# Causal masks written into the score banks first, and AV moved ahead of other work, in a two-layer transformer block

## The chip, the cores and the metric

One core of a Trainium2 chip runs the whole program in one launch. The metric is device time in microseconds, the median of several executions. TensorE multiplies matrices into PSUM banks (eight of them, 128 partitions by 512 fp32 columns), VectorE and ScalarE read those banks, GpSimd and the DMA queues move and prepare data. Each engine works through its own list of instructions in the order in which the program was recorded, and waits for other engines by semaphores.

## What is computed

The input is 8 sequences of 512 tokens with 256 features. Layer 0 is a layer norm, unmasked attention and a routed expert network beside it. Layer 1, which the change is about, is a layer norm, a causal attention that runs twice, and a low-rank network beside it:

```python
q, k, v = (qkv[:, :, 0], qkv[:, :, 1], qkv[:, :, 2])   # 16 heads of 16 features
ctx = _causal_attn(q, k, v)                            # softmax(mask(q k^T / 4)) v
ctx_c = ctx.reshape(b, s, d).transpose(0, 2, 1)
conv_out = conv(ctx_c, conv_w, width 3) + conv_b
q2 = conv_out.transpose(0, 2, 1).reshape(b, s, NUM_HEADS, HEAD_DIM)
ctx2 = _causal_attn(q2, k, v)
out = ctx2.reshape(b, s, d) @ out_w.T + out_b
```

The convolution is written in short here. In the causal attention, key positions later than the query get minus infinity before the softmax.

## The kernel before

**Jobs.** The attention is cut into jobs of one sequence and four heads. Layer 1 has 64 jobs: 32 for the first attention (`firsts`) and 32 for the second (`seconds`), which come in turn, the second behind the first by LAG = 7. A head has 16 features in a row group of 32 partitions, so four heads fill the 128 rows of TensorE, and matmuls of different heads use different 32-row tiles of it.

**Steps.** A job takes six steps in layer 1 (STEPS), and `run` (L442) goes through all steps of all jobs in one line. In every step two things are under way. The newer job gets the row maxima of its scores (`scores`, L332): queries on the partitions, two heads per step, all in fp32, and VectorE takes the maxima out of the banks (L365). Twelve steps later (LEAD) the same job gets its scores again (`exps`, L384), this time with keys on the partitions and the maxima already subtracted (a spare row of q holds them, written by `shift`, L372, by a transpose L375 and four small DMAs on SP's queue). ScalarE takes the exponentials out (L421). The query blocks of the maxima (MX_SEQ) and the key blocks of the scores (SC_SEQ) are paired so that they have equal widths: 512, then 384 and 128 in one bank, then 256, and the same again for the other two heads. `zip` (L482) puts the maxima matmuls of two heads (L345) and the score matmuls of the other two (L394) side by side, so that all four row tiles have work.

**Masks.** Keys of block kc are only scored for queries from block kc on (L389), so only the first 128 columns of each piece need a mask. `after` (L407) adds it: one bf16 matmul per head (L412) of an identity with `mask_t`, which holds -1e30 above the diagonal, onto the first `len(blocks)*128` columns. The pieces lie in the bank such that the masked columns come first: the piece with offset 0 is 128 wide where there are two. In this matmul TensorE works as one array of 128 rows.

**AV.** `attend` (L427) multiplies exponentials by values (L434), with the four heads on four 32-column tiles of TensorE. By AV_AT a job attends its key block 0 in the sixth step of its scores, blocks 1 and 3 in the next (the first step of the following job), block 2 in the one after it. After the last, `l1_done` (L1101) has ScalarE copy the result (L1106), and books its transposes into token order (`to_tokens`, L1090), which VectorE divides (L1093, L1094).

**Other work.** Projections of q and k (L293, emptied by VectorE at L283 and by ScalarE at L285), values (L303, L311), transposes into features (L266; emptied at L268 by VectorE and L270 by ScalarE), the convolution (L1072, in two halves, emptied by VectorE at L283), the output projection (L1124, added by VectorE at L1131) and `to_tokens` are booked in a list (`Work`) with an earliest and a latest step. In layer 1 `fill` (L118) takes at most one of them per step, more only if they are due.

**Order in a step.** Maxima and scores, masks, exponentials (issued to ScalarE), `fill`, then `attend`.

**Banks.** In layer 1 the rings are: three banks for maxima ("mx"), three for scores ("sc"), one for AV, one for all other work ("mm"). A step takes two of the three "mx" and two of the three "sc" banks. For the last LEAD steps `banks_last` hands the banks of the maxima to the scores.

Of the kernel before, what the change touches and what calls it, by code (L numbers as in the profile page):

```python
# [1 line left out]

# [17 lines left out]
P = 128  # L20
NB = 8
S = 512
# [5 lines left out]
PH = 32  # L28
# [46 lines left out]
SC_SEQ = (  # L75
    [((i // 2,), 1 - i % 2) for i in range(8)],
    [((0,), 0), ((3, 1), 0), ((2,), 0), ((0,), 1), ((3, 1), 1), ((2,), 1)],
    [((0,), 0), ((0,), 1), ((3, 1), 0), ((3, 1), 1), ((2,), 0), ((2,), 1)],
)
# [73 lines left out]
def block_kernel(ctx: ExitStack, tc: tile.TileContext, x, a0_wqk, a0_bqk, a0_wv, a0_bv, cent, experts,  # L153
                 a1_wqk, a1_bqk, a1_wv, a1_bv, conv_w, conv_b, out_w, out_b, u1, v1, f_b1, u2, v2, f_b2, out):
    nc = tc.nc
# [20 lines left out]
    ident_bf = const.tile([P, P], BF16, name="ident_bf")  # L176
    nc.vector.tensor_copy(ident_bf, ident)

    mask_t = const.tile([P, 2 * P], BF16, name="mask_t")
# [19 lines left out]
    def share_banks(**kinds):  # L199

        rings.update({k: list(v) for k, v in kinds.items()})

    def bank(kind="mm"):
        rings[kind].append(rings[kind].pop(0))
        return rings[kind][-1]
# [5 lines left out]
    def banks_alone():  # L211
        share_banks(mx=banks[:3], sc=banks[3:6], av=banks[6:7], mm=banks[7:])


    def banks_last():
        share_banks(sc=banks[:5], av=banks[6:7], mm=banks[5:6] + banks[7:])
# [4 lines left out]
    class Norms:  # L221
# [4 lines left out]
        def __init__(self, pool, bs, nm, twice):  # L226
            self.bs, self.nm, self.twice = bs, nm, twice
            n = len(bs) * NC
            self.mv = pool.tile([P, n, 2], F32, name=f"mv{nm}", bufs=1)
            self.rs = pool.tile([P, 2 if twice else 1, n], F32, name=f"rs{nm}", bufs=1)  # L230
            self.rs1 = pool.tile([P, n], F32, name=f"rs1{nm}", bufs=1) if twice else None
            self.nm2 = pool.tile([P, n], F32, name=f"nn{nm}", bufs=1) if twice else None
            self.nm_t = pool.tile([P, n], F32, name=f"nm{nm}", bufs=1)
# [85 lines left out]
    class Job:  # L319


        def __init__(self, nm, causal, scale, v, g, done, pool):
            self.nm, self.causal, self.scale, self.v, self.g, self.done = nm, causal, scale, v, g, done
            self.pool = pool
            self.q = self.k = None
            self.m = None
            self.seq = int(causal)
            self.shift_row = (HD, 0)[g % 2]
            self.e = {}
            self.av = None  # L330

        def scores(self, i):  # L332
# [39 lines left out]
        def shift(self):  # L372
# [8 lines left out]
            for c in range(NC):  # L381
                nc.sync.dma_start(out=self.q[self.shift_row : P : PH, c * P : (c + 1) * P], in_=mT[4 * c : 4 * c + 4, :])

        def exps(self, i):  # L384
            blocks, pr = SC_SEQ[self.seq][i]
            heads = [bank("sc") for _ in range(2)]
            parts, at = [], 0
            for kc in blocks:
                lo = kc * P if self.causal else 0  # L389
                parts.append((kc, at, lo))  # L390
                at += S - lo
            mm = [
                [
                    lambda h=h, kc=kc, at=at, lo=lo: nc.tensor.matmul(  # L394
                        heads[h % 2][:, at : at + S - lo],
                        lhsT=self.k[h * PH : (h + 1) * PH, kc * P : (kc + 1) * P],
                        rhs=self.q[h * PH : (h + 1) * PH, lo:],
                        start=kc == blocks[-1],
                        stop=not self.causal,
                    )  # L400
                    for h in (2 * pr, 2 * pr + 1)
                ]
                for kc, at, lo in reversed(parts)
            ]
            n = at

            def after():  # L407
                if self.causal:


                    for h in range(2):
                        nc.tensor.matmul(  # L412
                            heads[h][:, : len(blocks) * P], lhsT=ident_bf, rhs=mask_t[:, : len(blocks) * P],
                            start=False, stop=True,
                        )
                e = self.pool.tile(
                    [P, 2, n], F32, tag=f"e{blocks[0]}" if self.causal else "e", name=f"e{self.nm}_{i}",
                    bufs=3 if self.causal else 4,
                )
                for h in range(2):  # L420
                    nc.scalar.activation(e[:, h, :], heads[h][:, :n], AF.Exp, scale=self.scale)  # L421
                for kc, at, lo in parts:
                    self.e[kc, pr] = e[:, :, at : at + S - lo]

            return mm, after
# [16 lines left out]
    def run(jobs, work_of, layer, per_step, most):  # L442
        steps, lead = STEPS[layer], LEAD[layer]
        end = steps * len(jobs)
        if layer == 1:
            for job in jobs[-(lead // steps) :]:
                job.seq = 2
        attends = {}
        for j, job in enumerate(jobs):
            av_at = AV_AT[job.seq]  # L450
            for i, blocks in av_at.items():
                attends.setdefault(lead + steps * j + i, []).append((job, blocks, i == max(av_at)))

        def attend(t):
            for job, blocks, last in attends.pop(t, ()):
                for kc in blocks:
                    job.attend(kc, kc == 0, last and kc == blocks[-1])
                if last:
                    job.done(job, t)

        work_of.first()
        for t in range(max(attends) + 1):
            work_of.t = t
            if layer == 0 and t == lead:
                banks_alone()
            mm, after = [], []
            if t >= lead or layer == 1:
                maxima = (t,)
            else:

                maxima = (t, t + 1) if t % 2 == 0 else ()

            scores = (t - lead,) if t < end else (t - lead, t - lead + 1) if (t - end) % 2 == 0 else ()
            if t == end:
                banks_last()
            for at, call in [(i, Job.scores) for i in maxima] + [(i, Job.exps) for i in scores]:
                j, i = divmod(at, steps)
                if 0 <= j < len(jobs):
                    m, a = call(jobs[j], i)
                    mm.append(m)  # L480
                    after.append(a)
            for together in zip(*mm):  # L482
                for m in together:
                    for f in m:
                        f()
            for f in after:
                f()
            work_of.fill(t, per_step, most)
            attend(t)
        work_of.drain()  # L490

    fgs, yns, norms_of = {}, {}, {}
# [72 lines left out]
    with ExitStack() as l0:  # L565
# [335 lines left out]
        jobs = []  # L901
# [37 lines left out]
        for i in range(2):  # L939
            norms[1].stats(i)  # L940
        todo.stream = stream()
        run(jobs, todo, 0, MOE_PER_STEP, 99)
        later.close()

# [16 lines left out]
    with tc.tile_pool(name="ffn", bufs=1, side="right", reuse_waits="tile") as ffn:  # L961
# [53 lines left out]
        for n, (b, c2) in enumerate(pairs):  # L1015
# [6 lines left out]
            _, _, hT = ahead.pop(0)  # L1022
# [11 lines left out]
    for i in range(2):  # L1034
        t = l1.tile([P, 2, S + 2], F32, tag=f"ctxT{i}", name=f"ctxT{i}", bufs=1)
# [107 lines left out]
    firsts, seconds, jobs = [], [], []  # L1143
# [30 lines left out]
    for n in range(NB * HG + LAG):  # L1174
        if n < NB * HG:
            l1_job(1, n)
        if n >= LAG:
            l1_job(2, n - LAG)
    run(jobs, todo1, 1, 99.0, 1)


# [86 lines left out]
```

## Time and profile before

| | |
|---|---|
| median of 3 runs | 2121.69 us (2117.05 to 2124.36) |
| the profiled execution | 2120.86 us |
| its span in the trace | 2118.7 us |
| TensorE busy (PE) | 2010.6 us, 95% of the span |
| VectorE (DVE), ScalarE (ACT) | 1228.6 us, 867.8 us |
| layer 1's attention | from about 1140 us to the end |
| maxima matmuls L345 | 3072 passes, 765.1 us busy (both layers) |
| score matmuls L394 | 3072 passes, 682.6 us busy (both layers) |
| mask matmuls L412 | 768, 123.4 us busy |
| AV matmuls L434 | 3072 passes, 317.8 us busy (both layers) |

An fp32 matmul of the program is two instructions of the profile (two passes), each with a weight load (PEld) ahead of it; a bf16 one is one. Busy times of matmuls that run side by side overlap, and a matmul's recorded end lies behind the time at which the next one may start, so a stretch that shows TensorE at 99% can still hold waits: they are found in the timeline and in the list of waits. "issue" as a releaser means that nothing shown by the profile was waited for.

### The profile page before, as it was taken

To read this page: it belongs to the slowest core of one execution; us is meant where nothing else is said; L and a number is where in the kernel's file an instruction comes from. 1 tells how busy PE (TensorE), PEld (TensorE's weight loads), DVE (VectorE), ACT (ScalarE), POOL (GpSimd) and SP (SyncE) were. 2 spreads that over 40 slices of the span, in tenths; PEclk is the share of its full clock that TensorE was granted. 3 is DMA by queue.
4 is the path that set the end of the run, shared out by engine and by line. 5 is a ranking of instruction groups with operands and counts; after the bars stand their busy time and mean duration, and the time that the engine had idled before them with its cause. 6 is when DMAs were issued, how large, how long until landed. Compare 5 with 4: busy or idle time off the path is not lost.

```text
span 2118.7 us, 35530 instructions
## 1 busy us (share of the span) xinstructions
PE 2010.6 (95%) x13672; PEld 1016.4 (48%) x13672; DVE 1228.6 (58%) x3565; ACT 867.8 (41%) x1690; POOL 175.6 (8%) x222
## 2 busy tenths in 40 slices
PE   5797999999999999998898999999999999999998
PEld 3333555555555555552233445455555545554554
DVE  5564455555555555557424676666766666666763
ACT  4342333333333333335551444444444444444434
POOL 4153000000000000004211000000000000000000
PEclk8698999999999999999999899999999999999999
DMA  6014212212121221202100000000000000000000
GB/s 211 13 45 143 104 54 105 101 58 105 53 105 53 105 105 53 105 11 78 40 1 1 2 2 2 2 2 12 2 12 2 12 2 12 2 11 2 2 12 21
DMA packets 37192, 93.53 MB, mean 44 GB/s; under 512 B 5920, under 2 KB 28064, under 8 KB 34080
## 3 DMA queue, kind: packets, MB, share of 16 engines
q0 software_dynamic: 6384, 59.78, 7.7%
q1 hardware_dynamic: 29792, 30.56, 4.5%
q8 instruction: 107, 1.75, 0.3%
q10 hardware_dynamic: 848, 0.93, 0.1%
q14 instruction: 61, 0.50, 0.1%
HBM read 70.03 MB, written 20.45 MB: 43 GB/s over the span
## 4 chain that ended last, share of the span: by engine, by line
PE 83%; DVE 6%; issue 5%; DMA 4%; ACT 2%; POOL 1%; ACTq 0%; POOLq 0%; DVEq 0%; SPq 0%
PE bank L345 27%; PE bank L434 12%; PE bank L794 8%; PE bank L815 8%; PE bank L293 5%; PE bank L1072 4%; PE bank L412 4%; DMA hs_d<-h,pos_i 4%; PE bank L394 3%; PE bank L303 2%; PE bank L1090 2%; PE bank L1124 1%; DVE m L362 1%; PE bank L977 1%; PE bank L990 1%
## 5 line engine op out<-in xcount | busy, mean ns | idle before, releaser
L421 ACT ACTIVATE e<-bank 128x512 f32<-128x512 f32 (+1 forms) x1280 | 638.9, 552 | 921.4 <-PE bank L394 462.8
L345 PE MATMUL bank<-k,q 32*128 32x512 f32 (+3 forms) x3072 | 765.1, 538 | 24.6 <-DVE m L362 20.3
L394 PE MATMUL bank<-q,k 32*128 32x512 f32 (+3 forms) x3072 | 682.6, 535 | 2.4 <-DVE m L362 1.6
L365 DVE CUSTOM_DVE_ANT_0 jk<-bank,cmask 128x512 bf16<-128x512 f32 (+3 forms) x1024 | 502.8, 491 | 241.7 <-PE bank L345 162.4
L345 PEld LDWEIGHTS bank<-k,q 32*128 32x128 f32 x3072 | 301.4, 187 | 388.4 <-issue 165.2
L362 DVE TENSOR_REDUCE m<-bank 128x1 f32<-128x512 f32 x512 | 328.8, 685 | 152.5 <-PE bank L394 122.7
L434 PE MATMUL bank<-e,v 128*32 128x512 f32 (+3 forms) x3072 | 317.8, 501 | 0.7 <-ACT e L421 0.7
L394 PEld LDWEIGHTS bank<-q,k 32*128 32x128 f32 x3072 | 266.0, 186 | 12.2 <-issue 6.1
L794 PE MATMUL bank<-hsT,w 128*128 128x256 f32 x736 | 181.2, 392 | 6.4 <-DVE hsT L777 6.4
L794 PEld LDWEIGHTS bank<-hsT,w 128*128 128x128 f32 x736 | 135.1, 192 | 74.5 <-issue 58.9
L815 PE MATMUL bank<-w,hT 128*128 128x256 f32 x736 | 170.7, 385 | 0.0
L815 PEld LDWEIGHTS bank<-w,hT 128*128 128x128 f32 x736 | 137.5, 192 | 36.6 <-issue 18.7
L434 PEld LDWEIGHTS bank<-e,v 128*32 128x32 f32 x3072 | 67.7, 108 | 139.7 <-issue 133.0
L412 PE MATMUL bank<-mask_t,ident_bf 128*128 128x128 bf16 (+1 forms) x768 | 123.4, 244 | 0.0
L412 PEld LDWEIGHTS <-ident_bf 128*128 128x128 bf16 x768 | 43.9, 97 | 155.7 <-issue 140.6
L807 DVE TENSOR_SCALAR hT<-bank,w 128x256 f32<-128x256 f32 x92 | 44.5, 484 | 113.7 <-ACT hT L805 113.7
L1072 PE MATMUL bank<-ctxT,cw_sb 128*128 128x256 f32 x384 | 90.0, 383 | 2.1 <-DVE q L283 1.8
L365 DVE DVE_READ_ACCUMULATOR2_ANT m<- 128x1 f32 x1024 | 85.0, 83 | 0.0
L805 ACT ACTIVATE hT<-bank,w 128x256 f32<-128x256 f32 x92 | 43.7, 475 | 92.9 <-PE bank L794 92.9
L824 DVE TENSOR_TENSOR f<-bank,w 128x256 f32<-128x256 f32 x46 | 19.5, 425 | 105.4 <-PE bank L815 105.4
L285 ACT ACTIVATE k<-bank,bqk,rows 128x512 f32<-128x512 f32 x64 | 46.3, 774 | 81.7 <-PE bank L293 72.4
L1072 PEld LDWEIGHTS bank<-ctxT,cw_sb 128*128 128x128 f32 x384 | 70.1, 189 | 13.2 <-DVE q L283 3.2
(186 smaller groups left out, 1383.5 us busy)
## 6 DMA issues: line engine op xcount, KB each, us to landing
q<-mT SPq DMA_DIRECT2D x384, 2.0 KB
hs_d<-zeros SPq DMA_DIRECT2D x23, 256.0 KB
hs<-hs_d SPq DMA_DIRECT2D x23, 256.0 KB
fs_d<-f SPq DMA_DIRECT2D x23, 256.0 KB
acc<-in_x SPq DMA_DIRECT2D x8, 512.0 KB
out<-acc SPq DMA_DIRECT2D x8, 512.0 KB
cw_sb<-in_conv_w SPq DMA_DIRECT2D x1, 768.0 KB
wqk<-in_a_wqk ACTq DMA_DIRECT2D x1, 512.0 KB
```

What stands on the lines that cost most here:

```text
L285: nc.scalar.activation(dst, ps, AF.Identity, bias=bias[:, half : half + 1], scale=rows[:, half : half + 1])
L293: nc.tensor.matmul(ps, lhsT=w[:, k, col : col + P], rhs=src[:, k, :], start=(k == 0), stop=(k == 1))
L345: lambda h=h, qc=qc, at=at, nk=nk: nc.tensor.matmul(heads[h % 2][:, at : at + nk], lhsT=self.q[h * PH : (h + 1) * PH, qc * P : (qc + 1) * ...
L362: nc.vector.tensor_reduce(self.m[:, qc, h, :], src, AX.X, ALU.max, negate=True)
L365: nc.vector.tensor_tensor_reduce(out=junk[:, :nk], in0=src, in1=cmask[:, S - nk :], scale=1.0, scalar=-3e38, op0=ALU.add, op1=ALU.max, acc ...
L394: lambda h=h, kc=kc, at=at, lo=lo: nc.tensor.matmul(heads[h % 2][:, at : at + S - lo], lhsT=self.k[h * PH : (h + 1) * PH, kc * P : (kc + 1 ...
L412: nc.tensor.matmul(heads[h][:, : len(blocks) * P], lhsT=ident_bf, rhs=mask_t[:, : len(blocks) * P], start=False, stop=True,)
L421: nc.scalar.activation(e[:, h, :], heads[h][:, :n], AF.Exp, scale=self.scale)
L434: nc.tensor.matmul(self.av[h * PH : (h + 1) * PH, lo:], lhsT=self.v[:, kc, 4 * self.g + h, :], rhs=es[h // 2][:, h % 2, :], start=first, s ...
L794: nc.tensor.matmul(ps[:, i * TB : (i + 1) * TB], lhsT=w[:, O_W1 + k * FF + fc * P : O_W1 + k * FF + (fc + 1) * P], rhs=self.hsT[:, k, :], ...
L815: nc.tensor.matmul(ps[:, 0:D], lhsT=self.hT[:, fc, j * P : (j + 1) * P], rhs=w[:, O_W2 + fc * D : O_W2 + (fc + 1) * D], start=(fc == 0), s ...
L1072: nc.tensor.matmul(ps[:, :w], lhsT=cw_sb[:, k, tap, c * P : (c + 1) * P], rhs=ctxT[b % 2][:, k, tap + lo : tap + lo + w], start=(k == 0 an ...
```

## The change

Three things change in layer 1.

First, `masks` (new) runs at the end of each step and takes the two score banks of the next step. It writes the mask into them with `start=True`, ahead of the scores; `exps` finds these banks by `self.banks`. The scores then add to them (`start=False`).

Second, since the mask covers only some columns of the bank, each score matmul is cut at the end of its masked columns: one 128-wide piece on masked columns, one for the rest. A 512-wide matmul becomes 384 and 128, a 256-wide one 128 and 128; 384 and 128 become 256, 128 and 128. The lists of maxima and scores now differ in length, so `zip` becomes `zip_longest`, and the last score pieces stand alone at the end. Per job that is 28 score matmuls in place of 16. The mask matmuls stay 12 per job.

Third, up to the last LEAD steps, `attend` comes ahead of `fill`. The order in a step is then: maxima and scores, exponentials, AV, other work, the masks of the next step. `banks_last` moves from the start of step `end` to the end of the step before it.

In layer 0 the instructions and their order stay what they were, and on every engine but TensorE layer 1's order stays too, except that ScalarE's copy of a finished AV is now issued ahead of the same step's other work.

```diff
+        def masks(self, i):
+            n = len(SC_SEQ[self.seq][i][0]) * P
+            self.banks[i] = heads = [bank("sc") for _ in range(2)]
+            for h in heads:
+                nc.tensor.matmul(h[:, :n], lhsT=ident_bf, rhs=mask_t[:, :n], start=True, stop=False)
+
         def exps(self, i):
             blocks, pr = SC_SEQ[self.seq][i]
-            heads = [bank("sc") for _ in range(2)]
+            heads = self.banks.pop(i) if self.causal else [bank("sc") for _ in range(2)]
...
+            pieces = [(kc, at, lo, S) for kc, at, lo in parts]
+            if self.causal:
+                pieces = [(kc, at, lo, lo + P) for kc, at, lo in parts]
+                pieces += [(kc, at + P, lo + P, S) for kc, at, lo in parts if lo + P < S]
             mm = [
                 [
-                    lambda h=h, kc=kc, at=at, lo=lo: nc.tensor.matmul(
-                        heads[h % 2][:, at : at + S - lo],
+                    lambda h=h, kc=kc, at=at, lo=lo, hi=hi: nc.tensor.matmul(
+                        heads[h % 2][:, at : at + hi - lo],
                         lhsT=self.k[h * PH : (h + 1) * PH, kc * P : (kc + 1) * P],
-                        rhs=self.q[h * PH : (h + 1) * PH, lo:],
-                        start=kc == blocks[-1],
-                        stop=not self.causal,
+                        rhs=self.q[h * PH : (h + 1) * PH, lo:hi],
+                        start=not self.causal,
+                        stop=at == 0,
                     )
                     for h in (2 * pr, 2 * pr + 1)
                 ]
-                for kc, at, lo in reversed(parts)
+                for kc, at, lo, hi in reversed(pieces)
             ]
...
             def after():
-                if self.causal:
-                    for h in range(2):
-                        nc.tensor.matmul(
-                            heads[h][:, : len(blocks) * P], lhsT=ident_bf, rhs=mask_t[:, : len(blocks) * P],
-                            start=False, stop=True,
-                        )
...
-            for together in zip(*mm):
+            for together in zip_longest(*mm, fillvalue=()):
                 for m in together:
                     for f in m:
                         f()
             for f in after:
                 f()
+            early = layer == 1 and t < end
+            if early:
+                attend(t)
             work_of.fill(t, per_step, most)
-            attend(t)
+            if not early:
+                attend(t)
+            if t + 1 == end:
+                banks_last()
+            for at in scores_at(t + 1) if layer == 1 else ():
+                j, i = divmod(at, steps)
+                if 0 <= j < len(jobs):
+                    jobs[j].masks(i)
```

`scores_at(t)` is the old expression for the steps whose scores belong to t, made a function.

More of the change, by code (lines that the diff above doesn't have):

```diff
@@ L1 @@
 from contextlib import ExitStack
+from itertools import zip_longest
 import concourse.bass as bass
@@ L329, in __init__ @@
             self.e = {}
+            self.banks = {}
             self.av = None
@@ L391, in exps @@
                 at += S - lo
+            n = at
+            pieces = [(kc, at, lo, S) for kc, at, lo in parts]
+            if self.causal:
+                pieces = [(kc, at, lo, lo + P) for kc, at, lo in parts]
+                pieces += [(kc, at + P, lo + P, S) for kc, at, lo in parts if lo + P < S]
             mm = [
                 [
-                    lambda h=h, kc=kc, at=at, lo=lo: nc.tensor.matmul(
-                        heads[h % 2][:, at : at + S - lo],
+                    lambda h=h, kc=kc, at=at, lo=lo, hi=hi: nc.tensor.matmul(
+                        heads[h % 2][:, at : at + hi - lo],
                         lhsT=self.k[h * PH : (h + 1) * PH, kc * P : (kc + 1) * P],
-                        rhs=self.q[h * PH : (h + 1) * PH, lo:],
-                        start=kc == blocks[-1],
-                        stop=not self.causal,
+                        rhs=self.q[h * PH : (h + 1) * PH, lo:hi],
+                        start=not self.causal,
+                        stop=at == 0,
                     )
@@ L402, in exps @@
                 ]
-                for kc, at, lo in reversed(parts)
+                for kc, at, lo, hi in reversed(pieces)
             ]
-            n = at
             def after():
-                if self.causal:
-                    for h in range(2):
-                        nc.tensor.matmul(
-                            heads[h][:, : len(blocks) * P], lhsT=ident_bf, rhs=mask_t[:, : len(blocks) * P],
-                            start=False, stop=True,
-                        )
                 e = self.pool.tile(
@@ L459, in attend, with scores_at @@
                     job.done(job, t)
+        def scores_at(t):
+            return (t - lead,) if t < end else (t - lead, t - lead + 1) if (t - end) % 2 == 0 else ()
         work_of.first()
@@ L471, in run @@
                 maxima = (t, t + 1) if t % 2 == 0 else ()
[L473 to L476, printed above, removed]
+            for at, call in [(i, Job.scores) for i in maxima] + [(i, Job.exps) for i in scores_at(t)]:
                 j, i = divmod(at, steps)
```

## The prediction

> **What bounds the kernel now.** I first read the busy time by stretches (engine columns are busy us and instruction counts), then the waits of the layer-1 stretch, then the timeline step by step.
>
> ```profile
> 1190.00:2085.00 895.00, 887.08 (x7706) 466.45 (x7698) 609.61 (x2275) 402.64 (x833) 0.00 (x0) 1.00 0.02 6
> ...
> PEld bank L345 <- DVE m L365: 55.8, 113, 0.8
> ...
> PEld bank L1090 <- ACT avs L1106: 11.1, 39, 0.4
> ```
>
> In steady layer 1 (1190 to 2085 us) TensorE is busy for 887 of 895 us, VectorE 610, ScalarE 403. ScalarE waits 431 us for the masks (L412), but that is slack: exponentials are read two or more steps later. What TensorE waits for is the maxima on VectorE (55.8 us), then the copied AV or a freed work bank. The prize is small: everything TensorE waits for in layer 1 is some 80 to 90 us, and masks and scores keep their columns.
>
> The timeline repeats every six steps with only a few kinds of each, so I measured each kind's length from the slot of one mask pair to the next (the slot follows the last score matmul) and counted them. I call the steps 0 to 5 by the score pieces of SC_SEQ: 0 and 3 are 512 wide, 1 and 4 are 384+128, 2 and 5 are 256. AV falls in steps 0, 1 and 5. A step without AV or other work (step 3 of a job, TensorE rows, the last but two from ScalarE):
>
> ```profile
> 1608.74 0.28 PE L412 MATMUL bank<-mask_t,ident_bf 128*128 128x128 bf16 x2
> 1608.96 1.14 PE L345 MATMUL bank<-k,q 32*128 32x384 f32 x3
> 1609.52 0.79 PE L394 MATMUL bank<-q,k 32*128 32x384 f32 x2
> 1609.72 0.69 PE L345 MATMUL bank<-k,q 32*128 32x128 f32 x3
> 1609.94 0.68 PE L394 MATMUL bank<-q,k 32*128 32x384 f32 x2
> 1610.78 0.39 PE L412 MATMUL bank<-mask_t,ident_bf 128*128 128x256 bf16 x2
> ...
> 1609.07 1.08 ACT L421 ACTIVATE e<-bank 128x512 f32<-128x512 f32 x2 [1.39 <-PE bank L412]
> ```
>
> The second maxima matmul waits for VectorE until 1609.51; the second score matmul waits for the first exponential until 1609.72. And step 1 with other work:
>
> ```profile
> 1617.12 0.39 PE L412 MATMUL bank<-mask_t,ident_bf 128*128 128x256 bf16 x2
> ...
> 1617.35 1.88 PE L293 MATMUL bank<-yT,wqk 128*128 128x512 f32 x4
> ...
> 1619.16 0.64 PE L434 MATMUL bank<-e,v 128*32 128x256 f32 x8
> 1619.28 1.53 DVE L283 TENSOR_SCALAR q<-bank,rows,bqk 128x512 f32<-128x512 f32 x2
> ...
> 1620.38 0.28 PE L412 MATMUL bank<-mask_t,ident_bf 128*128 128x128 bf16 x2
> ...
> 1620.95 0.63 PE L1090 MATMUL bank<-ident,avs 128*128 128x128 f32 x4 [0.28 <-DVE q L283]
> ...
> 1622.58 0.28 PE L412 MATMUL bank<-mask_t,ident_bf 128*128 128x128 bf16 x2
> ```
>
> Projection, AV (0.57 to the next scores), scores, next work; from mask pair to mask pair step 1 is 3.26 us here and step 2 2.20. There is one work bank ("mm"), and AV lies between the projection and the next user (L1090), covering part of VectorE's 1.53 us of emptying it.
>
> **The pieces.** 768 score matmuls are added (12 a job, 64 jobs), each two fp32 passes with a weight load; columns stay the same. Four 32-row tiles run side by side. Splitting already exists before: a 4x512 group takes 1.07 us to its masks, 4x384 then 4x128 takes 1.08, since the later loads run under the passes. In each new step the score tiles stream as many columns as the maxima tiles, so I take 0. The Trainium skill speaks against it: "TensorE: Matmul & The Clock Gate", "Step-by-step: what each phase is for", says matmuls stay in program order and only weight loads are pulled ahead. By that, the trailing 128-wide pieces (two passes, 0.22 us) would run after the longer maxima: 384 steps x 0.22 = 84 us. But in the fence the 128-wide L345 starts at 1609.72, ahead of the second passes (1609.94) of matmuls issued before it: tiles don't wait for one another. Bounds 0 and 84; I go with the row.
>
> **Masks and switches.** In steps with neither AV nor work, or AV alone, the mask pair costs 0.217 us (128 wide) or 0.325 (256) between a row-tiled group and its neighbour; moving it to the other side of AV leaves that unchanged. With other work behind the masks before, the next weight load ran under them (work starts 0.07 or 0.125 after them). After, the work's load is exposed and the mask's is covered.
>
> Step 0 (62 jobs in the trace's regular part): before, 0.07 to the transpose L375, 0.255 to AV, AV 1.00, next scores 1.08: 2.41. After, AV 1.00, transpose 0.12, a mask pair now for step 1, so 256 wide (0.21+0.09), scores 1.08: 2.50. +0.09 x 62 = +5.7 us. Some of it is paid back in step 1: with work (36 jobs) AV 0.57, work (projection 1.81), masks 0.20, scores 0.64 = 3.23 against 3.26, -1.2 us in all.
>
> The new wait: the second mask of a pair needs the bank of the first head just scored (three "sc" banks), so it waits for that head's exponential; maxima, scores and all else queue behind it on TensorE. Before, the exponential started 0.33 us (step 4: 0.38) after the score end, 0.10 behind the mask's recorded end; after, 0.10 behind the last score pass's end: 0.15 and 0.16. It lasts 0.60, and its release took 0.05 more (1609.67 to 1609.72). The second mask runs at 0.80, and scores can start at about 0.96 (128 wide) or 1.00 (256).
> - Step 1 with AV alone (25 jobs): 0.96, but VectorE holds the second maxima until 1.04 (before and after): 0. Its L1090 then waits less for the AV copy, but VectorE holds the next step too (before at 0.98, after the same): 0.
> - Step 3, empty (22) or with a short work item (22): the scores' wait ended at 0.98; now 1.00, and row 1.08: 2.075 against 2.04, +0.035 x 44 = +1.5. The maxima come out later too, so an empty step 4 behind it (15) loses 0.03: +0.5. Behind a projection in step 3 (16), exposed load and wide masks, +0.12: +2.0. Step 4 otherwise: VectorE's 1.04 exceeds 0.96, and work hides it: about -0.7 in all.
>
> **AV ahead of other work.** This is the largest term. In step 1 the work bank's emptying starts 0.57 us (AV) later relative to TensorE's other work. Take the projection (14 jobs). Before: L1090's weight load came 1.755 us after the projection's end (1619.16 to 1620.92): VectorE's two passes over the bank start 0.12 after it, take 1.53, and the release 0.11. Steps 1 and 2 took 3.26+2.20 = 5.46. After: projection ends at 0.57+1.92 = 2.49 after the score end, L1090 still 1.755 later: 4.24; then transposes 0.48, masks 0.20, scores 1.07: 5.99. +0.54 x 14 = 7.6, plus 0.5 for step 1's credit counted above: 8.0. The same sum for values (L303, 7 jobs; emptied 0.98 after the end): +0.17 each, 1.2. Output (L1124, 12; accumulation ends after 0.95 to 0.98): +0.18 or, before a convolution, +0.27: 2.6. Convolution (3): +0.4 to +0.5, 1.4. Together +13.2.
> In step 5 it helps: the second convolution half waited 0.52 us behind the masks for VectorE's emptying (8 jobs; 5.37 us) or 0.33 for ScalarE's copy (6), values or output 0.33 (6). AV (1.00) first hides this: 4.95 against 5.37, -0.42 x 8; -0.23 x 12: -6.1 us.
> In step 0, shift's four DMAs on SP leave 1 us later; they land within 2.2 us (L382 x4), 12 us before use: 0. ScalarE's AV copy moves ahead of work's k copies: 0. No order on VectorE, GpSimd or SP changes. The last twelve steps are bound by exponentials that start about 0.3 earlier: -1.
>
> **Sum.** 5.7 - 1.2 + 2.0 + 2.0 - 0.7 + 13.2 - 6.1 - 1 = +13.9; I take +14. The profiled execution took 2120.86 us (span 2118.7), 0.8 under the median 2121.69; on the median, 2135.5, rounded to 2135.
>
> **Rivals.**
> - Gain: scores no longer wait behind an exponential, and neither the new mask wait nor the later emptying counts. Then step 3 gains 0.21 x 22 and some 0.15 x 22, step 4 0.17 x 15, L1090's shorter wait 0.1 x 25, step 5 6.1, the end 1; about 20, less 3 for exposed loads: 2104. For it: ScalarE starts 0.17 to 0.22 earlier everywhere. Against: VectorE's 1.04 and the one work bank don't move. It decides when the exponential ends before the mask's turn, that is with over 0.8 us of work between. 16%.
> - Little net effect: step 2's extra 0.54 is taken back in step 4, where VectorE is waited for 0.72, if VectorE is not pushed back as well. Then 14 - 7.6 = +6: 2128, down to no change. Against: its emptying delays its maxima equally. 20%.
> - Pieces cost: part of the 84 us; a third gives 2135 + 28 = 2163. 8%.
> - My forecast, 2135, own range 2128 to 2148: 56%.
>
> A measurement of this kernel tells about 0.3% (6.4 us) from no change: faster 16%, within 20%, slower 64%. From 2113 to 2155 leaves out most of the gain rival and of the pieces rival, some 2 in 10.
>
> **What would show it.** Right: TensorE waits at the new mask line for exponentials in steps 1, 3 and 4; L1090 (L1107 after) waits about 1 us behind step-1 projections; step 5's convolution wait is gone; a score group still lasts 1.07, 1.08, 0.64; step 0 grows to 2.50. Wrong: groups longer by 0.1 to 0.2 (pieces), scores starting before 0.9 in empty steps, or layer 1 shorter.

## The result and the profile after

The changed kernel takes 2146.42 us (median of 6 runs, 2141.74 to 2154.54) where the kernel before takes 2120.48 beside it (6 runs). The ratio is 1.0134 [1.0104, 1.0164], which is 28 us slower (the two medians differ by 26). I had forecast 14 slower, with a range of 2128 to 2148 us, so the time lies at its upper end. The profiled execution took 2154.54 us, its span is 2152.8. From layer 1's first maxima matmul to the end it has 1007.8 us where before had 979.3: +28.5. The other 5.5 us of the two spans lie in layer 0, whose instructions are the same; up to layer 1's first mask my profiled kernels differ by up to 15 us (1164.7 to 1180.1), so in what follows I compare layer 1, step by step. That is one profiled execution of each kernel.

The same stretch as before, by busy time (columns as before: PE, PEld, DVE, ACT, POOL, granted clock, DMA share, GB/s):

```profile
1190.00:2085.00 895.00, 831.72 (x8873) 521.11 (x8867) 591.36 (x2201) 387.22 (x805) 0.00 (x0) 0.99 0.02 6
```

TensorE is now idle for 63 of 895 us in the records, where it was 8, and VectorE and ScalarE got less done in the same time (591 against 610, 387 against 403). No engine became the bound: there is more waiting. For what, the list of waits of this stretch says (us in total, times, longest):

```profile
PEld bank L347 <- DVE m L367: 63.8, 82, 1.2
...
PE bank L392 <- ACT e L428: 37.3, 58, 0.9
...
PEld bank L1107 <- ACT e L428: 15.5, 14, 1.1
...
PE bank L1107 <- ACT e L428: 12.3, 13, 0.9
...
PEld bank L1107 <- ACT avs L1123: 6.9, 24, 0.3
```

Line 1 is the old wait for the maxima, 63.8 against 55.8. Line 2 is new: the second mask of a pair waits for an exponential. Lines 3 and 4 are the transposes into token order behind a projection; before, TensorE's row for these 14 read 4.0 us and named VectorE's emptying (L283). Here an exponential is named, and it is not what is waited for, as the timeline below shows. Line 5 fell from 11.1 to 6.9, as forecast.

The step that the prediction showed first, step 3 with neither AV nor work, of the same job (TensorE and ScalarE):

```profile
1612.61 0.39 PE L410 MATMUL bank<-q,k 32*128 32x128 f32 x4
1612.92 0.28 PE L392 MATMUL bank<-mask_t,ident_bf 128*128 128x256 bf16 x1
1613.79 0.27 PE L392 MATMUL bank<-mask_t,ident_bf 128*128 128x256 bf16 x1 [0.58 <-ACT e L428]
1613.99 0.59 PE L347 MATMUL bank<-k,q 32*128 32x384 f32 x2
1614.00 0.70 PE L410 MATMUL bank<-q,k 32*128 32x256 f32 x4
...
1614.87 0.28 PE L410 MATMUL bank<-q,k 32*128 32x128 f32 x2
1615.08 0.70 PE L1089 MATMUL bank<-ctxT,cw_sb 128*128 128x256 f32 x2
...
1613.14 1.09 ACT L428 ACTIVATE e<-bank 128x512 f32<-128x512 f32 x2 [1.33 <-PE bank L410]
```

The first mask is written at 1612.92 into the free third bank. The second needs the bank of the head just scored. Its exponential starts at 1613.14, ends 0.60 later, and the mask follows at 1613.79; all else of TensorE stands behind it. Before, the first maxima and scores ran in this gap (maxima from 0.22 after the slot, which is the start of the first mask); now nothing does until 1.07. The step takes 2.158 us, before 2.035.

Step 1 with a projection and the step 2 behind it:

```profile
1638.52 0.64 PE L441 MATMUL bank<-e,v 128*32 128x256 f32 x8
...
1639.09 1.99 PE L294 MATMUL bank<-yT,wqk 128*128 128x512 f32 x4
...
1640.91 0.28 PE L392 MATMUL bank<-mask_t,ident_bf 128*128 128x128 bf16 x2
1641.12 1.53 DVE L284 TENSOR_SCALAR q<-bank,rows,bqk 128x512 f32<-128x512 f32 x2 [0.57 <-PE bank L294]
1641.12 0.49 PE L347 MATMUL bank<-k,q 32*128 32x256 f32 x2
...
1642.02 0.66 ACT L428 ACTIVATE e<-bank 128x256 f32<-128x256 f32 x2 [1.69 <-PE bank L410]
...
1642.79 0.63 PE L1107 MATMUL bank<-ident,avs 128*128 128x128 f32 x4 [0.95 <-ACT e L428]
1643.25 0.28 PE L392 MATMUL bank<-mask_t,ident_bf 128*128 128x128 bf16 x2
```

VectorE frees the work bank at 1642.65 and the transposes start 0.14 later; the exponentials named as releaser end at 1642.68 and touch none of their tiles (the experiment that gives the transposes another bank settles it). Step 2 takes 2.765, before 2.201. And the second half of the convolution in step 5, before and after:

```profile
1596.70 0.99 DVE L283 TENSOR_SCALAR q<-bank,rows,cb_sb 128x256 f32<-128x256 f32 x2 [1.18 <-PE bank L1072]
...
1597.24 0.28 PE L412 MATMUL bank<-mask_t,ident_bf 128*128 128x128 bf16 x2
...
1597.75 2.86 PE L1072 MATMUL bank<-ctxT,cw_sb 128*128 128x256 f32 x12 [0.23 <-DVE q L283]
```

```profile
1617.98 1.00 DVE L284 TENSOR_SCALAR q<-bank,rows,cb_sb 128x256 f32<-128x256 f32 x2 [0.88 <-PE bank L1089]
...
1618.63 1.07 PE L441 MATMUL bank<-e,v 128*32 128x512 f32 x8
...
1619.63 2.86 PE L1089 MATMUL bank<-ctxT,cw_sb 128*128 128x256 f32 x12
```

AV stands in the gap and the wait is gone: 4.975 us for the step, before 5.369.

I measured every step of the 370 regular ones of layer 1 in this way, from the end of its last score pass to that of the next step's, in both traces. Predicted and measured, each summed over its steps:

| term | predicted | measured |
|---|---|---|
| step 0 (2.404 to 2.515 us, 61 steps) | +5.7 | +6.7 |
| step 1 | -1.2 | +0.4 |
| step 2, late emptying of the work bank | +13.2 | +11.7 |
| step 3 (empty 2.035 to 2.158, with short work to 2.193, behind a projection 3.066 to 3.221) | +3.5 | +8.7 |
| step 4 (to 1.706) | -0.2 | +1.6 |
| step 5 | -6.1 | -5.6 |
| two stretches at half clock in steps 4 and 5 | none | +3.0 |
| end, and the first steps of layer 1 | -1 | +2.0 |
| sum | +13.9 | +28.5 |

### The profile page after: what moved, and what is told of

Same layout as the page of the kernel before. It is cut to its first block, busy times and chain, and to the rows that moved or that the text cites. A ratio compares the mean times of both kernels' runs of the same rounds, so it can differ in the third digit from the quotient of the medians.

```text
span 2152.8 us, 38538 instructions
## 1 busy us (share of the span) xinstructions
PE 1984.1 (92%) x15208; PEld 1092.6 (51%) x15208; DVE 1230.5 (57%) x3565; ACT 864.8 (40%) x1690; POOL 174.9 (8%) x222
## 4 chain that ended last, share of the span: by engine, by line
PE 80%; ACT 8%; DVE 6%; DMA 3%; issue 3%; POOL 0%; DVEq 0%; ACTq 0%; SPq 0%; POOLq 0%
PE bank L347 21%; PE bank L441 12%; PE bank L811 8%; PE bank L832 8%; PE bank L410 7%; PE bank L294 5%; ACT e L428 5%; PE bank L1089 4%; PE bank L392 3%; DMA hs_d<-h,pos_i 3%; PE bank L304 2%; DVE m L364 2%; PE bank L1107 2%; PE bank L1141 1%; PE bank L994 1%
## 5 line engine op out<-in xcount | busy, mean ns | idle before, releaser
L428 ACT ACTIVATE e<-bank 128x512 f32<-128x512 f32 (+1 forms) x1280 | 638.8, 552 | 1001.4 <-PE bank L410 964.0
L347 PE MATMUL bank<-k,q 32*128 32x512 f32 (+3 forms) x3072 | 720.7, 538 | 23.9 <-DVE m L364 20.6
L410 PE MATMUL bank<-q,k 32*128 32x128 f32 (+3 forms) x4608 | 675.0, 412 | 2.4 <-DVE m L364 1.6
L347 PEld LDWEIGHTS bank<-k,q 32*128 32x128 f32 x3072 | 267.4, 188 | 337.8 <-issue 110.5
L410 PEld LDWEIGHTS bank<-q,k 32*128 32x128 f32 x4608 | 349.6, 188 | 44.1 <-issue 4.7
L392 PE MATMUL bank<-mask_t,ident_bf 128*128 128x128 bf16 (+1 forms) x768 | 141.2, 240 | 47.8 <-ACT e L428 40.7
L392 PEld LDWEIGHTS <-ident_bf 128*128 128x128 bf16 x768 | 64.0, 98 | 86.7 <-issue 69.0
```

The source lines that it names most:

```text
L347: lambda h=h, qc=qc, at=at, nk=nk: nc.tensor.matmul(heads[h % 2][:, at : at + nk], lhsT=self.q[h * PH : (h + 1) * PH, qc * P : (qc + 1) * ...
L392: nc.tensor.matmul(h[:, :n], lhsT=ident_bf, rhs=mask_t[:, :n], start=True, stop=False)
L410: lambda h=h, kc=kc, at=at, lo=lo, hi=hi: nc.tensor.matmul(heads[h % 2][:, at : at + hi - lo], lhsT=self.k[h * PH : (h + 1) * PH, kc * P : ...
```

## The experiments

Each run is timed beside the kernel before. "Steps" is the sum over layer 1's regular steps of one profiled run against the trace of before; it doesn't contain layer 0's spread, so it is the sharper of the two, but it rests on one execution of each kernel, and a change of up to some 4 us in it can come from the first jobs of layer 1, where the length of a stretch at half clock differs between traces. The microseconds behind a ratio are worked out from the ratio; the difference of the two medians can lie some 2 us away.

**Which part costs what.** Three kernels take the change apart. The first is the changed kernel with AV behind the work again:

```diff
-            early = layer == 1 and t < end
+            early = False
```

> The changed kernel with AV put back behind the other work; masks still ahead, scores still in pieces. Theory: AV ahead of the work delays the emptying of the one work bank; that costs the changed kernel about 11.6 us in step 2 and earns 5.7 us in step 5. Both go here, so this kernel lies about 20 us over the kernel before, 6 under the changed one, and step 2 behind a projection falls from 2.76 to about 2.2 us. Rival (the masks' wait for the exponentials carries nearly all of the loss): 25 to 28 us over the kernel before, step 2 still near 2.7.

Measured: 2153.42 us (6 runs), ratio 1.0161 [1.0134, 1.0188], +34; steps +31.2. Neither theory has it: without AV ahead the kernel is slower still. Step 2 behind a projection did fall (2.765 to 2.090), as I held, and the gain of step 5 went (5.472). But step 0 rose from 2.515 to 2.622 and step 1 with work from 3.252 to 3.359, 0.107 in each of some 97 steps. Step 0 of this kernel, then of the changed one:

```profile
1216.76 0.28 PE L377 MATMUL bank<-ident,m 128*16 128x128 f32 x1
1216.97 1.07 PE L441 MATMUL bank<-e,v 128*32 128x384 f32 x16
...
1217.97 0.39 PE L392 MATMUL bank<-mask_t,ident_bf 128*128 128x256 bf16 x2
1218.29 0.59 PE L347 MATMUL bank<-k,q 32*128 32x384 f32 x2
```

```profile
1212.28 1.07 PE L441 MATMUL bank<-e,v 128*32 128x384 f32 x16
...
1213.28 0.28 PE L377 MATMUL bank<-ident,m 128*16 128x128 f32 x1
1213.39 0.38 PE L392 MATMUL bank<-mask_t,ident_bf 128*128 128x256 bf16 x2
1213.71 0.59 PE L347 MATMUL bank<-k,q 32*128 32x384 f32 x2
```

Between the row-tiled scores and the column-tiled AV, the transpose of full height (L377) takes 0.21 us; between AV and the mask, itself of full height, it takes 0.11. Counting the order in the program, work ahead of AV makes one change more between kinds of tiling when the masks stand at the end of a step. (Whether the change itself takes this time or the weight load that it leaves uncovered, no run separates.) The early masks are what makes AV ahead of work worth having.

The second is the kernel before with AV ahead of other work and nothing else:

```diff
+            early = layer == 1 and t < end
+            if early:
+                attend(t)
             work_of.fill(t, per_step, most)
-            attend(t)
+            if not early:
+                attend(t)
```

> The kernel before with AV alone moved ahead of the other work; masks and scores as before. Theory: step 2 behind a projection grows from 2.20 to about 2.67 us (late emptying), steps with AV and work pay a further switch of tiling since masks, AV and work now stand in three modes (about 0.12 us in step 0, 0.2 in step 1), step 5 with work gains 0.1 to 0.3: about 21 us over the kernel before. Rival (the order of AV and work is harmless, all of the loss comes from the masks): 0 to 4 us.

Measured: 2141.92 us (6 runs), ratio 1.0104 [1.0076, 1.0131], +22; steps +21.8, as expected. Step 0 2.502, step 1 with work 3.455 (+0.195; step 0 rises by 0.098; one more change of tiling in each), step 2 behind a projection 2.768, step 5's convolution 5.073.

The third has only the cut: score matmuls in two pieces, masks behind them as before.

```diff
-                for kc, at, lo in reversed(parts)
+                for kc, at, lo, hi in reversed(pieces)
...
-            for together in zip(*mm):
+            for together in zip_longest(*mm, fillvalue=()):
```

> The kernel before with its scores cut into the same pieces, masks behind the scores and AV behind the work as before. Theory: row tiles don't wait for one another, a group of matmuls gets 0.01 us longer: 0 to 4 us over the kernel before. Rival (matmuls of different tiles keep the program's order, or the further weight loads count): 0.1 to 0.2 us a step, 38 to 84 us.

Measured: 2121.2 us (14 runs), ratio 1.0006 [0.9987, 1.0025]; steps +2.2. A group of scores lasts about 0.010 longer than before and no more. Strict program order (38 to 84 us) is out for these tiles.

So the parts alone give +2.2 (cut), +21.8 (AV ahead), +31.2 (early masks with the cut), and all together +26.5. They don't add: AV ahead costs 21.8 with late masks and gives 4.7 back with early ones.

**Bank or VectorE?** The token transposes get AV's bank, which is free at that time, in place of the work bank:

```diff
-        ps = bank()
+        ps = bank("av")
```

First in the changed kernel:

> The changed kernel with one edit: the transposes into token order use the AV bank, which is free between the copy of a finished AV and the next job's first AV, and no longer the work bank. Theory (late emptying of the work bank): step 2 behind a projection falls from 2.76 to about 1.9, behind values or output to 1.85; 10 to 13 us under the changed kernel, 14 to 17 over the kernel before. Rival (these steps are long for another reason, VectorE's backlog): as the changed kernel, about 26 over the kernel before.

Measured: 2143.1 us (6 runs), ratio 1.0105 [1.0075, 1.0135], +22; steps +18.9. Between my theory and the rival:

```profile
1633.52 1.53 DVE L284 TENSOR_SCALAR q<-bank,rows,bqk 128x512 f32<-128x512 f32 x2 [0.57 <-PE bank L294]
...
1634.18 0.66 PE L1107 MATMUL bank<-ident,avs 128*128 128x128 f32 x4
...
1634.67 0.41 PE L392 MATMUL bank<-mask_t,ident_bf 128*128 128x128 bf16 x2
1634.97 0.41 DVE L367 CUSTOM_DVE_ANT_0 jk<-bank,cmask 128x256 bf16<-128x256 f32 x1
...
1635.01 1.12 PE L347 MATMUL bank<-k,q 32*128 32x512 f32 x2
1635.45 0.59 PE L410 MATMUL bank<-q,k 32*128 32x384 f32 x2
```

The transposes no longer wait (they start while VectorE still empties the projection), so the work bank was what held them. But VectorE gets to the maxima only at 1634.97 and has read their bank at 1635.39; the second maxima matmul and the scores behind it stand until 1635.44 (L410 is the first score of the step). Step 2 falls to 2.335, not to 2.2: of its growth of 0.564, 0.430 was the bank, the rest VectorE behind the late emptying.

Then in the kernel before, alone:

> The kernel before with the transposes into token order in the AV bank; nothing else. Theory (one work bank, emptied late by VectorE): step 2 behind a projection gets shorter, but VectorE, which has the emptying ahead of the maxima, then holds the next group, so 2.20 falls to about 2.0 only: 3 us under the kernel before, too little for the medians to tell, to be read in the steps. Rival (the work bank never held these transposes): step 2 stays at 2.20.

Measured: 2116.88 us (22 runs), ratio 0.9984 [0.9968, 0.9999]; step 2 behind a projection falls from 2.201 to 1.883 (14 steps, -4.4 us), more than the 2.0 that I expected; nothing else in the regular steps grew. (Its steps sum to -8.8; the other 4.4 lie in the first jobs of layer 1, where the trace of before runs at half clock for 20.5 us, from 1168 to 1189, and this one for 6.8, from 1160 to 1167.)

**Only where something covers the wait.** From the changed kernel, the early mask is written only in steps with AV or with other work in between that is booked at over 1 us; elsewhere the mask comes behind the uncut scores as before.

```diff
-            heads = self.banks.pop(i) if self.causal else [bank("sc") for _ in range(2)]
+            ahead = i in self.banks
+            heads = self.banks.pop(i) if ahead else [bank("sc") for _ in range(2)]
...
+            busy = t in attends or t + 1 >= end
...
+            busy = busy or work_of.done > 1.0
-            for at in scores_at(t + 1) if layer == 1 else ():
+            for at in scores_at(t + 1) if layer == 1 and busy else ():
```

> The changed kernel, with masks ahead of the scores (and scores in pieces) only where AV or long work lies between the two steps; behind steps 3 and 4 without AV or with short work, the masks follow uncut scores as in the kernel before. Theory (the second mask waits for an exponential that ends about 0.8 us after the scores, and so holds TensorE in these steps; the idle time also brings the half-clock windows): step 3 empty back from 2.16 to 2.04, with short work from 2.19 to 2.04, step 4 empty from 1.71 to about 1.66, no half-clock window within layer 1: 8 to 11 us under the changed kernel, about 16 over the kernel before. Rival (masks cost the same wherever they stand; the switches between tilings are the price): no gain over the changed kernel, 26 over the kernel before.

Measured: 2144.81 us (6 runs), ratio 1.0121 [1.0082, 1.0160], +26; steps +26.0. Half of it came as expected: step 3, empty or with short work, is at 2.035 again, empty step 4 at 1.66 to 1.67 in 30 of 37, and layer 1 beyond its first jobs runs at full clock. But by steps the kernel is only 0.5 better than the changed one, with the half clock's 3.0 in it, and the time shows no gain, as the rival had it. For step 5 with AV alone rose from 2.292 to 2.510 in 40 of its 41 steps:

```profile
1625.38 0.28 PE L428 MATMUL bank<-mask_t,ident_bf 128*128 128x128 bf16 x2
1625.60 1.06 PE L450 MATMUL bank<-e,v 128*32 128x512 f32 x8
...
1626.60 0.28 PE L394 MATMUL bank<-mask_t,ident_bf 128*128 128x128 bf16 x2
1626.81 0.70 PE L349 MATMUL bank<-k,q 32*128 32x512 f32 x2
```

Where a late mask (L428) meets the next step's early one (L394), both pairs lie in one step, each at 0.22 us between its neighbours. So it is in step 5 with work, in step 4 with the convolution (3.556 to 3.686) and in step 3 behind a projection (3.221 to 3.297); together these steps took back some 12 us, and step 2, which loses a pair, gave 3.7. I had counted the waits taken away, not the second mask pair. The rival's reason is half right: the waits do have a price, and so have the mask pairs.

With the tokens in AV's bank besides:

> Masks ahead only where covered, and token transposes in the AV bank: the two remedies for the changed kernel together, AV still ahead of work in every step. Theory (late emptying and the masks' wait are separate terms): the two gains add up, 8 us for the bank and 8 to 11 for the masks: 6 to 10 us over the kernel before, what is left being the wide masks and exposed weight loads of step 0 and of VectorE's backlog behind projections in step 2. Rival (they are one and the same wait seen twice): no better than the better of the two, 15 to 20 over.

Measured: 2139.86 us (7 runs), ratio 1.0094 [1.0055, 1.0133], +20; steps +19.0, where the tokens in AV's bank alone had +18.9. The rival has the time right, but not the reason: the bank takes 7.0 us out of the steps here and 7.6 without the covered masks, so the two are not one wait seen twice. It is the covered masks that bring nothing. Step 2 behind a projection stays at 2.330, on VectorE.

**Is there a faster version?** The kernel before with tokens in AV's bank, and the changed order only at step 5 (written as an edit of the kernel above):

```diff
-            early = layer == 1 and t < end
+            early = layer == 1 and t < end and [x[1] for x in attends.get(t, ())] == [(0,)]
+            busy = early
```

> The kernel before, with AV ahead of work, and masks ahead of scores, only in step 5 (where the work waits for its bank or its input and a block-0 AV of 1.0 us covers that), and the transposes into token order in the AV bank. Theory: step 5 with work gains what it gained in the changed kernel, 5.7 us, step 2 gains 3 us, nothing else moves by more than 0.01 us a step: 8 us under the kernel before (ratio 0.996). Rival (each part of the change costs wherever it is applied): at or over the kernel before.

Measured: 2121.49 us (14 runs), ratio 1.0003 [0.9982, 1.0024]. Step 0, rid of its mask, fell from 2.404 to 2.287 in 61 steps (-7.0), but step 5 with AV alone took it back, 2.284 to 2.510 in 41 (+9). It is the same doubled mask as above. It also ate what step 5 with work was to gain: the convolution takes 5.193 here, values and output 4.328. So the masks stay late, and only AV moves, only there:

```diff
+            early = layer == 1 and t < end and [x[1] for x in attends.get(t, ())] == [(0,)]
+            if early:
+                attend(t)
             work_of.fill(t, per_step, most)
-            attend(t)
+            if not early:
+                attend(t)
...
-        ps = bank()
+        ps = bank("av")
```

> The kernel before (late, unsplit masks) with the token transposes in AV's bank, and AV ahead of other work only in the sixth step of the scores (step 5), where the convolution's second half, values or output wait for an emptied bank. My theory: the gains add. Tokens in AV's bank took 8.8 us out of the steps (3.6 us of the medians); AV ahead in step 5 took 0.30 from each of 8 convolution steps, 0.11 from each of 12 others, 3.7 us together, where it was done in every step, and step 0 stays at 2.40 since its AV stays behind. So 12 to 13 us under the kernel before by steps, 7 to 12 in the medians (ratio 0.994 to 0.997). Rival: the later emptying of the work bank in step 5 comes out in step 0 or 1 behind it (a longer wait for the maxima), and the time is that of tokens in AV's bank alone (ratio 0.998).

Measured: 2119.7 us (22 runs) beside 2123.05 of the kernel before (27), ratio 0.9977 [0.9958, 0.9996]. By steps the gains add as the theory says: step 5's convolution 5.369 and 5.186 to 5.073, its other work 4.325 to 4.209 (-3.7), step 2 -4.4, step 0 at 2.403; -12.2 with the first jobs of layer 1, of which 4.1 are again the shorter half-clock stretch. By the ratio it is 5 us (1 to 9), by the two medians 3.4, less than the 7 to 12 that I expected. The ratio is the rival's 0.998, and its interval overlaps that of the tokens alone: a gain on the kernel before is measured, one on the tokens alone is shown only in the steps.

## Why the prediction was right in kind and half in size

**The work bank (+13.2, measured +11.7).** Right, to 0.01 us a step in the largest class: step 2 behind a projection was worked out as 2.76 and took 2.765. The bank experiment splits the growth: 0.43 of 0.56 us is the bank, and 0.13 VectorE would have held anyway behind the same emptying, which is what the prediction said against "little net effect". The sum was 1.5 too high: the steps behind AV alone, put at nothing, got 0.7 shorter, and those behind the output projection gave 1.8 where 2.6 was forecast.

**Step 5 (-6.1, measured -5.6).** Right, its longer convolution step was worked out as 4.95 and took 4.975.

**Step 0 (+5.7, measured +6.7).** Right, 2.50 forecast, 2.515 taken. That the transpose gets cheaper beside a mask was in the sum, and the first experiment shows that this, with the same in step 1, is over half of what AV ahead brings once the masks are early (9.8 of 17.3 us, against 12.6 lost in step 2).

**Steps 3 and 4 (+3.3, measured +10.3).** Here is the first mis-sized term. The step was: the exponential starts "0.10 behind the last score pass's end: 0.15 and 0.16", so scores start at 0.96 to 1.00. Measured in the fence above: exponential 0.22 after the slot, second mask 0.87, scores 1.07. I had carried the distance from a bf16 mask's recorded end (0.10) over to an fp32 pass, where it is 0.16 (1612.98, where the first head's last pass ends in the fence's first row, to 1613.14). Release and width of the masks were right (0.05 and 0.20). With 0.07 more the new wait ends behind VectorE's 1.04, which I had counted on as a floor, so that it also decides in step 4 (1.706 in all but the convolution's), in step 1 with AV alone (+0.6 us) and in all 44 short steps 3. A wait that comes out within 0.1 us of the one that it replaces should have had 0.1 us in the range for every step where it falls, some 120 of them. The experiment that leaves the masks late in the empty and short steps gave nearly all of it back there (step 3 from +6.2 to about 0, step 4 from +1.5 to +0.6), though not in the time, as shown above.

**The cut (0, measured 0.010 a group, +2.2 alone).** Right to choose the row over the page: "TensorE: Matmul & The Clock Gate" of the Trainium skill ("Step-by-step: what each phase is for") would have made 84. Zero was still a little low: the cut adds 0.01 to a group.

**Step 1 (-1.2, measured +0.4).** The credit with work was 0.005 a step where I had 0.03. The cut alone makes this step 0.012 longer; the rest of the difference wasn't taken apart.

**Half clock (+3.0).** Not in the prediction at all:

```profile
1506.00:1509.90 3.90, 2.64 (x40) 1.58 (x32) 2.90 (x12) 1.90 (x4) 0.00 (x0) 1.00 0.02 4
1509.90:1513.40 3.50, 3.50 (x27) 1.42 (x30) 1.73 (x8) 0.93 (x3) 0.00 (x0) 0.52 0.00 0
1513.40:1517.00 3.60, 3.60 (x55) 2.27 (x59) 1.65 (x6) 1.08 (x2) 0.00 (x0) 1.00 0.00 0
```

After an empty step 3 and an empty step 4, in which TensorE is busy for 2.64 of 3.90 us, it runs at a granted clock of 0.52 for some 3.5 us. The stretch costs 1.5 us, 1.1 of it in step 5. This trace has two such stretches in layer 1 beyond its first jobs, so have the two other kernels whose masks wait in every empty step, and the eight in which no early mask waits there (that of before among them) have none. The changes of the clock in all the traces lie on a grid of 3.41 us. I cut the steady part of layer 1 of all eleven traces along it, some 2,900 windows. Each of the six half-clock windows follows one in which TensorE is busy for only 62 to 63%: for 2.15 of 3.41 us from 1506.60 on, and again from 2086.86 on, in this trace. No window that is busy for 68% or more is followed by half clock, and only these three kernels have windows below that, 13 in all; before has none below 91%, and the kernel with late masks in these steps none below 72%. Seven of the 13 were not followed by half clock either, at 63 to 66%; what decides among them stays open. So in these traces the half clock never came without the new idle time, but the idle time does not bring it each time: 12 of the 14 pairs of an empty step 3 and an empty step 4 here keep full clock. Each kernel has one profile.

**The end (-1).** Not gained: from the last step 0 on, 30.4 us before and 30.5 after. Of the 2.0 us in the table 1.6 lie in the first jobs of layer 1 and weren't taken apart; the kernel with only the cut has 4.4 us more there than before has, so they need not be the change's.

**The rivals.** The gain fails as I said, on the one work bank and VectorE's time. "Little net effect" counted on step 4 to take back what step 2 loses; step 4 grew. The forecast's mechanisms stand. Of 15 us missed, 7 are the new wait, which was in the sum but too short, 3 the half clock and 3 the end and the first jobs, which were not in it or were put at a gain; the rest is small and partly cancels.

## What to carry to other kernels

A matmul placed ahead of time into a ring of banks waits for the reader of the bank it needs, and everything behind it on TensorE waits with it: find the moment that bank comes free, to 0.1 us, in every kind of step, and compare it with the wait that is there already. Count the changes between row tiles, column tiles and full height as instructions with a price of their own (0.1 us in three places here, 0.2 in a fourth), and count them for the whole order, since two moves that each add one can share it. Where an order is to change only in some steps, price the seam: a step that ends in the new order and began in the old one can carry the moved work twice.

## What the runs showed of the hardware beyond what was expected

- The half clock came with waits of 0.6 to 0.7 us among work. "TensorE: Matmul & The Clock Gate", Part 1 ("The HAM clock gate"), has the clock halve after an idle window of some 3.4 us; here no such window was idle: TensorE was busy for 62 to 63% of the 3.41 us ahead of each of the six half-clock windows. The length, about 3.4 us, agrees.
- An order with one more change between kinds of tiling took 0.107 us more in steps 0 and 1 alike with early masks, and with late ones 0.098 in step 0 and 0.195 in step 1. "TensorEngine Tiling (Array Packing)", "Key Properties", says that the engine drains then; no run here shows the drain by itself.
- In an empty step 3 an exponential starts 0.16 us behind the recorded end of its head's last fp32 score pass of 128 columns, and 0.10 behind that of a bf16 mask.
